# Zero fills, bias loads and the last image's attention reordered in a four-image vision-transformer kernel

## The chip, the cores and the metric

The kernel runs on one core of a Trainium2 chip. The metric is the device time of one execution in microseconds, the median of three runs. The core has engines with instruction streams of their own: TensorE (PE: matmuls and transposes, with weight loads PEld), VectorE (DVE), ScalarE (ACT), GpSimd (POOL) and SyncE (SP, which here only starts DMA transfers). An engine takes its instructions in order and waits at semaphores for the others.

## The reference

Four images of 3 x 224 x 224 pixels become 784 tokens each (patches of 8 x 8), of width 256, in float32:

```python
# tokenizer: patches -> (4, 784, 192)
tokens = layernorm(patches, ln1_g, ln1_b) @ W1 + b1
tokens = layernorm(tokens, ln2_g, ln2_b)
tokens = concatenate([tokens, tokens, tokens], axis=1)   # used 3 times
h = silu(layernorm(tokens @ Wp1 + bp1, lnp_g, lnp_b)) @ Wp2 + bp2
# layer 0: at each token position attention between the images, 8 heads of 32
mn = layernorm(layernorm(h)) * gamma + beta
q, k, v = mn @ Wq, mn @ Wk, mn @ Wv
g = sigmoid(mn @ Wg + bg)
att = softmax(einsum('slhc,tlhc->sth', q, k) * scale, axis=1)
h = h + (einsum('sth,tlhc->slhc', att, v) * g) @ Wo + bo
# layer 0: two experts of six per token, chosen by a router
x = layernorm(h)
p = softmax(relu(x @ router_w1 + router_b1) @ router_w2 + router_b2)
w = softmax(top2(p))
h = h + sum(w_e * (relu(relu(x @ w1_e + b1_e) @ w2_e + b2_e) @ w3_e + b3_e))
# layer 1: linear attention with W_qkv and W_out, then a shared MLP
# plus two experts of four per token
```

The shape of the tokens after the concatenation is (4, 2352, 256). As the three parts are equal, and as nothing tells them apart later, the kernel computes 784 rows for each image and writes each result three times. `s` and `t` number images: an image's query meets the keys of all four images, its products summed over all positions.

## The kernel before

An image has six tiles of 128 tokens and 16 left over; the 64 left over of all images make tile 24, so 25 tiles. `h` holds all tokens in SBUF throughout.

**Patch section** (lines 330 to 526). The pixels land in `img` (126 partitions: rows of patches). Per group `k` of four patch columns (7 groups), `flatten(k, put)` copies pixels into patch order (`vT`, L342); `patch_stats` takes batch-norm statistics from `img` on DVE (L448); `patch_stds` turns them into a root, written into `vT` by ACT (L459); `turn_patches(k, c)` transposes `vT` on PE into `ptp` (L352) and copies it to `pT` (L356), c=0 for the first 128 pixels of a patch, c=1 for the other 64 and the root. In between stand the pieces of a generator (`steps`, begun by `next`), which folds W1, the norms and Wp1 into one weight `Wall`: pwct and pw/pwc (matmuls), the copy to the second half of `Wall` (L430), its end with `lastf` (L432 to L438), and `bp1` added (L441). Last, `pc` (L525) transposes `stage`, the 46 rows of biases and gains that 13 small loads bring (L178), and `cols` (L526) keeps them as columns. The order of this section on each engine is written out by hand.

**Tokenizer** (L612 to 730). `tokenize(g)` and `first_steps(g)` take tiles in groups: `pw` (L622) multiplies a tile with `Wall` in one c=0 and one c=1 pass for each half, ACT copies it, DVE takes statistics, and so on.

**GpSimd's and SyncE's queues in the front.** GpSimd issues the load of `bp1`, the 13 loads of `stage`, then memsets (`pL` L335, `nothing` L553, `base0` L575, `table` L581 and L587, `blk` L592, `shift`), then loads bp2, bo, rb2. SyncE issues images and weights and then 46 DMAs which write `nothing` over `xrows` and `yrows` in DRAM (L557; up to 896 KB each, 41 MB in all); each has a manual dependency on `turned`, the copy to `cols`.

**Layer 0.** `products(s, o, ts)` multiplies queries of image s with keys (`kq`) on DVE (L884); `gate_mm` (pg), `gate_act`, `shares_before/after` (the softmax over the images), `first_value` and `values` (weighted sums of v, `oT`, L930) and `attended(s, two)` (pwo, L291, `h` L959) follow. Then per part of the tokens: `rows_of_part` and `turn_part` normalise and transpose (`xn`, `pt`), `router` and `router_logits` (pr, `rT` L1019, plg L1030), `choose` (top two, a run of small DVE instructions), `count` (pcount), `send` (positions, then GpSimd scatters the rows to `xrows`, ordered by expert, L1121). The parts are `past` (image 1), `u` (image 2), `ua` and `ub` (image 3's two halves).

**Expert blocks.** When the rows of enough images are counted, `early_blocks()` finds 7 full blocks of 256 rows that are already known (ptotal, pplace, pmeta: places, experts). `load(i)` fetches block i from `xrows` to `xb` (L1437, after the scatters), `own_weights(i)` copies its expert's weights out of `ew` (all six experts, 1,540 columns each) with an offset read from a register (L1456, L1458), `turned(i)` transposes (ptb), `hidden(i, k)` multiplies (pb, L1482), `rows_back(i)` gives pyb (L1500) and writes to `yrows`; later rows are fetched back and added.

**The last image** (L1517 to 1640) is a list written out by hand, in whose order the instructions of each engine stand; `manual_schedule(engines=by_hand)` names the engines for which that holds. `ew` takes the place of `kq` when the products are done, and is loaded by 6 DMAs of 768 KB, each for all experts:

```python
        for i, name in enumerate(("expert_w1", "expert_w2", "expert_w3")):
            for c in range(2):
                nc.sync.dma_start(
                    out=ew[:, :, (2 * i + c) * D : (2 * i + c + 1) * D],
                    in_=a[f"L0_ffn_{name}"].rearrange("e (c p) n -> c p e n", p=P)[c],
                )
        for i in range(4):
            load(i)
```

After it come the second layer's attention and MLPs, which are not touched.

Of the kernel before, what the change touches and what calls it, by code (L numbers as in the profile page):

```python
# [27 lines left out]
P = 128  # L28
TT = 128
# [43 lines left out]
def tile_vit_tower(ctx: ExitStack, tc: tile.TileContext, a: dict, out: bass.AP):  # L73
# [97 lines left out]
    img = tokp.tile([IP, CY, WID], F32, tag="img", name="img")  # L171
    bp1 = tokp.tile([TT, D], F32, tag="bp1", name="bp1")
    nc.gpsimd.dma_start(out=bp1, in_=a["L0_tok_bp1"].partition_broadcast(TT))
# [3 lines left out]
    for src, n, width in plan:  # L177
        nc.gpsimd.dma_start(out=stage[r0 : r0 + n, :width], in_=src)  # L178
        r0 += n
# [153 lines left out]
    pT = tokp.tile([P, 2, QP, HP], F32, tag="pT", name="pT")  # L333
    pL = tokp.tile([P, 2, NI, SEG], F32, tag="pL", name="pL")
    nc.gpsimd.memset(pL, 1.0)  # L335
# [4 lines left out]

    def flatten(k, put):
        put(  # L342
            flat[:, k * PW : (k + 1) * PW, :PD].rearrange("q w (y x) -> q w y x", x=PATCH),
            img[:, :, k * PW * PATCH : (k + 1) * PW * PATCH].rearrange(
                "q y (w x) -> q w y x", x=PATCH
            ),
        )

# [12 lines left out]
    def first_layers():  # L361
# [12 lines left out]
        bb = tokp.tile([P, 2, TT], F32, tag="bb", name="bb")  # L374
        W1g = tokp.tile([KP, 2, D], F32, tag="W1g", name="W1g")
        W2 = tokp.tile([P, 2, D], F32, tag="W2", name="W2")
# [36 lines left out]
        WcT = tokp.tile([P, 2, 2 * P], F32, tag="WcT", name="WcT")  # L413
# [16 lines left out]
        nc.vector.tensor_copy(Wall[:, :, D:], pp)  # L430
# [9 lines left out]
        )  # L440
        nc.vector.tensor_tensor(bp1, pw, bp1, ALU.add)  # L441
# [21 lines left out]
    Wall = tokp.tile([P, 2, 2 * D], F32, tag="Wall", name="Wall")  # L463
    perm = tokp.tile([KP, 2, 2 * P], F32, tag="perm", name="perm")
# [7 lines left out]
    with tc.manual_schedule(engines=by_hand):  # L472
# [19 lines left out]
        cut0 = 5  # L492
        flatten(0, nc.vector.tensor_copy)
# [4 lines left out]
        flatten(3, nc.vector.tensor_copy)  # L498
        flatten(2, nc.scalar.copy)
        turn_patches(1, 0)  # L500
        next(steps)
# [3 lines left out]
        flatten(4, nc.scalar.copy)  # L505
        next(steps)
        turn_patches(3, 0)
        flatten(5, nc.scalar.copy)
        turn_patches(4, 0)
        patch_stds(0, cut0)  # L510
        turn_patches(5, 0)
        flatten(6, nc.scalar.copy)
        for k in range(2):
            turn_patches(k, 1)
        turn_patches(6, 0)
        for k in range(cut0, NK):
# [27 lines left out]
    rb2 = spread(wts, "rb2", a["L0_ffn_router_b2"])  # L544
    for put in weight_loads:
# [6 lines left out]
    nothing = tokp.tile([P, 7 * D], F32, tag="nothing", name="nothing")  # L552
    nc.gpsimd.memset(nothing, 0.0)  # L553
    for r in range(0, XROWS, 7 * P):
        n = min(7, (XROWS - r) // P)
        for rows_ in (xrows, yrows):
# [5 lines left out]
                put.ins, turned.ins.name,  # L562
# [15 lines left out]
    NQ = QMAX * E0  # L578
    table = const.tile([1, 5, NQ], F32, tag="table", name="table")
    for q in range(QMAX):  # L580
        nc.gpsimd.memset(table[:, 0, q * E0 : (q + 1) * E0], float(BLK * q))  # L581
    by_e = table.rearrange("r k (q e) -> r k q e", e=E0)
    for e in range(E0):
        for k, v in (
            (1, CAP * e - DUMMY), (2, EW * e), (3, D * e), (4, CAP * e - DUMMY + SMALL)
        ):
            nc.gpsimd.memset(by_e[:, k, :, e], float(v))  # L587
# [1819 lines left out]
```

## Time and profile before

| what | before |
|---|---|
| median of 3 runs | 746.83 us (746.51 to 748.01) |
| profiled execution | 774.73 us, its span 773.0 us |
| busy: PE, PEld | 702.5 us (91%), 479.4 us (62%) |
| busy: DVE, ACT, POOL | 475.7 (62%), 333.9 (43%), 126.2 us (16%) |
| moved by DMA | 96.49 MB, mean 125 GB/s |

The profile is one execution and is 27.9 us (3.7%) longer than the median. Engine rows name the line, engine, operation, output and input, the busy time, and in brackets the idle time before it with what ended it. In the row of slices each digit is a fortieth of the span (19.3 us) in tenths of busy time; PEclk is the clock granted to TensorE in tenths of full speed. In a row of waits the three numbers are the sum, the count and the longest.

### The profile page before, as it was taken

What the parts mean: (1) busy time and instruction counts of PE and PEld (TensorE: products, weight loads), DVE (VectorE), ACT (ScalarE), POOL (GpSimd) and SP (SyncE); (2) the same over time, 40 slices, a digit from 0 to 9 for tenths busy, and PEclk for the clock granted to TensorE, in tenths of its full rate; (3) what the DMA queues carried; (4) which work ended last, traced back from release to release, by engine and by line L of the source; (5) the groups of instructions that cost most, each with busy time, mean ns of one, the idle gap of its engine ahead of it and who ended that gap; (6) DMA issues with size and microseconds to landing.
All of it is one profiled execution on the core that took longest, in us unless ns stands there. A gap on an engine that the chain in (4) does not pass through costs nothing.

```text
span 773.0 us, 9815 instructions
## 1 busy us (share of the span) xinstructions
PE 702.5 (91%) x3005; PEld 479.4 (62%) x3005; DVE 475.7 (62%) x1487; ACT 333.9 (43%) x794; POOL 126.2 (16%) x232
## 2 busy tenths in 40 slices
PE   6889889999977778998899998789999999999996
PEld 4546555666655566787788874547776765554553
DVE  5686785869987553456444767348986844444541
ACT  1565766556674552342222326325446422222221
POOL 7200000000074226400003026724000000000000
PEclk9999999999998889999999998879999999999999
DMA  5799997000022913422324252312000012322333
GB/s 177 232 426 424 426 424 312 1 0 1 0 82 90 376 72 117 136 82 77 95 90 123 96 158 69 96 34 70 7 0 1 5 27 94 97 60 89 106 113 106
DMA packets 56284, 96.49 MB, mean 125 GB/s; under 512 B 6504, under 2 KB 46158, under 8 KB 56232
## 3 DMA queue, kind: packets, MB, share of 16 engines
q1 hardware_dynamic: 49732, 79.68, 28.8%
q0 software_dynamic: 5600, 14.32, 6.1%
q10 hardware_dynamic: 900, 1.86, 0.8%
q8 instruction: 24, 0.39, 0.2%
q14 instruction: 28, 0.23, 0.1%
HBM read 30.75 MB, written 65.09 MB: 124 GB/s over the span
## 4 chain that ended last, share of the span: by engine, by line
PE 68%; DVE 17%; ACT 7%; issue 4%; DMA 2%; DVEq 1%; another core or an unknown queue 1%; ACTq 0%
PE pb L1482 11%; PE pe L280 6%; PE pyb L1500 5%; PE ps L280 4%; PE pqk L1948 4%; PE pkv L280 4%; PE pt L271 4%; PE pw L622 3%; PE ps L2357 3%; PE pwp L291 3%; PE pukx L2047 3%; PE pout L2127 3%; DVE oT L930 3%; PE pout L2132 3%; DMA img<-in_x_dram 2%
## 5 line engine op out<-in xcount | busy, mean ns | idle before, releaser
L1121 POOL DMA_INDIRECT xrows<-xn,pos x50 | 53.0, 1061 | 246.4 <-DVE nm L980 189.4
L1705 POOL DMA_INDIRECT ys<-yrows,pos x50 | 49.1, 982 | 160.4 <-DMA yrows<-yb 126.7
L1482 PE MATMUL pb<-xTb,own 128*128 128x256 f32 (+1 forms) x240 | 55.8, 378 | 11.7 <-DVE own L1458 6.9
L1488 ACT ACTIVATE hb<-pb,own 128x256 f32<-128x256 f32 (+1 forms) x74 | 33.6, 457 | 62.6 <-PE pb L1482 51.3
L1948 PE MATMUL pqk<-Wqkv,lxT 128*128 128x512 f32 x100 | 49.9, 646 | 6.6 <-issue 6.6
L1482 PEld LDWEIGHTS pb<-xTb,own 128*128 128x128 f32 x240 | 42.3, 197 | 20.1 <-ACT hb L1488 7.8
L1500 PE MATMUL pyb<-own,hb 128*128 128x256 f32 x216 | 52.7, 384 | 0.3 <-ACT hb L1488 0.2
L1482 PE MATMUL pb<-hb,own 128*128 128x256 f32 (+1 forms) x240 | 52.1, 359 | 0.9 <-DVE hb L1490 0.6
L280 PE MATMUL pe<-xT,eW 128*128 128x512 f32 (+1 forms) x112 | 46.0, 553 | 0.0
L1500 PEld LDWEIGHTS pyb<-own,hb 128*128 128x128 f32 x216 | 40.8, 193 | 6.6 <-ACT hb L1488 0.6
L1482 PEld LDWEIGHTS pb<-hb,own 128*128 128x128 f32 x240 | 40.6, 190 | 5.8 <-DVE hb L1490 1.0
L1506 DVE TENSOR_TENSOR yb<-pyb,eb 128x512 f32<-128x512 f32 (+1 forms) x30 | 19.1, 638 | 39.1 <-PE pyb L1500 26.5
L622 PE MATMUL pw<-Wall,pT 128*128 128x512 f32 (+1 forms) x96 | 42.7, 593 | 0.0
L1471 ACT COPY xTb<-ptb 128x512 f32<-128x512 f32 (+1 forms) x30 | 16.2, 542 | 59.3 <-PE ptb L1467 49.3
L271 PE MATMUL pt<-ident,xn 128*128 128x128 f32 x200 | 30.4, 284 | 10.6 <-DVE xn L648 6.5
L271 PEld LDWEIGHTS pt<-ident,xn 128*128 128x128 f32 x200 | 23.8, 143 | 25.4 <-issue 6.2
L1490 DVE TENSOR_SCALAR hb<-pb,own 128x256 f32<-128x256 f32 (+1 forms) x46 | 20.5, 446 | 28.7 <-PE pb L1482 19.6
L1948 PEld LDWEIGHTS pqk<-Wqkv,lxT 128*128 128x128 f32 x100 | 19.9, 207 | 28.6 <-issue 26.8
L884 DVE SCALAR_TENSOR_TENSOR prod<-kq 128x784 f32<-128x784 f32 x32 | 30.4, 970 | 6.1 <-ACT kq L1298 3.4
L280 PEld LDWEIGHTS pe<-xT,eW 128*128 128x128 f32 x112 | 20.2, 190 | 21.6 <-issue 16.5
L1458 DVE COPY own<-ew 128x1540 f32 x30 | 28.9, 965 | 7.0 <-issue 2.6
L622 PEld LDWEIGHTS pw<-Wall,pT 128*128 128x128 f32 (+1 forms) x96 | 17.9, 189 | 20.0 <-issue 17.9
(420 smaller groups left out, 1469.1 us busy)
## 6 DMA issues: line engine op xcount, KB each, us to landing
xrows<-nothing SPq DMA_DIRECT2D x22, 896.0 KB
yrows<-nothing SPq DMA_DIRECT2D x22, 896.0 KB
out_dram<-h SPq DMA_DIRECT2D x23, 384.0 KB
xb<-xrows SPq DMA_DIRECT2D x24, 256.0 KB
yrows<-yb SPq DMA_DIRECT2D x24, 256.0 KB
ew<-in_L_ffn_expert_w_dram SPq DMA_DIRECT2D x6, 768.0 KB
wb<-wd SPq DMA_DIRECT2D x16, 128.0 KB
img<-in_x_dram SPq DMA_DIRECT2D x5, 294.0 KB
```

The lines of the kernel that those rows point to most:

```text
L271: nc.tensor.transpose(pt[:, j * TT : (j + 1) * TT], xn[:, j, c * P : (c + 1) * P], ident[:TT, :TT])
L280: nc.tensor.matmul(pm[: wcols.stop - wcols.start, :n], w[:, c, wcols], xT(c), start=(c == 0), stop=(c == chunks - 1),)
L291: nc.tensor.matmul(pm[:, i, :], xT(c, t), w[:, c, :], start=(c == 0), stop=(c == chunks - 1))
L622: nc.tensor.matmul(pm, pixels(c, tiles[j]), Wall[: K1[c], c, :], start=(c == 0), stop=(c == 1))
L884: nc.vector.scalar_tensor_tensor(prod, qTs[s][:, o, :], 1.0, kT[:, o, t * SEQ : (t + 1) * SEQ], ALU.mult, ALU.mult, accum_out=atts[s][:, o ...
L1121: put = nc.gpsimd.indirect_dma_start(out=xrows[:, :], out_offset=bass.IndirectOffsetOnAxis(ap=pos[:, k, t0 + j : t0 + j + 1], axis=0), in_ ...
L1458: nc.vector.tensor_copy(w, ewf[0][:, bass.ds(off, EW)])
L1482: nc.tensor.matmul(pm, wm[:, c, o * P : (o + 1) * P], src[:, c, :], start=(c == 0), stop=(c == 1),)
L1488: nc.scalar.activation(dst[:, o, :], pm, AF.Relu, bias=b)
L1500: nc.tensor.matmul(pm[:, t, :], src[:, c, t * P : (t + 1) * P], wm[:, c, :], start=(c == 0), stop=(c == 1),)
L1705: got = nc.gpsimd.indirect_dma_start(out=y[:, j, k, :], out_offset=None, in_=yrows[:, :], in_offset=bass.IndirectOffsetOnAxis(ap=pos[:, k, ...
L1948: nc.tensor.matmul(pqk, xTs[u][:, c, cut(j, 1)], Wqkv[:, c, : 2 * D], start=(c == 0), stop=(c == 1),)
```

## The change

- GpSimd's memsets go ahead of the load of `bp1`; the tiles made before them are named earlier, so that `nothing` and the others keep their addresses. The 13 loads of `stage` go behind bp2, bo and rb2 on GpSimd's queue and wait for DVE's last copy of `flatten`.
- `pc` and the copy to `cols` go from the end of the patch section into the tokenizer, ahead of group 1 (on PE behind the eight pw of the first pair).
- Groups 0, 3 and 5 of `flatten` are on DVE (before: 0 and 3), the other four on ACT. The second half of `Wall` is copied by ACT (before: DVE), and the last `pT` by ACT (before: DVE). 8 and 10 transposes of the identity whose result is not used are added on PE.
- The 46 zero fills wait for the last statistics of the pixels, no longer for `cols`.
- Last image: both `gate_mm` stand ahead of the products; `early_blocks` is cut into more pieces, placed apart; `ew` is a view of `kq`, loaded in 18 DMAs of 256 KB by expert, of which the first 6 come behind `products(3, 0, [3])`; `load` 0 to 3 come behind the first values; `router(u)` comes ahead of the values; `turned(0)`, `own_weights(0)`, `hidden(0, 0)` and `own_weights(1)` come ahead of `choose(u)`; `count(u)` comes behind `router(ua)`.

```diff
@@ -169,13 +169,48 @@
...
+    pT = tokp.tile([P, 2, QP, HP], F32, tag="pT", name="pT")
+    bb = tokp.tile([P, 2, TT], F32, tag="bb", name="bb")
+    W1g = tokp.tile([KP, 2, D], F32, tag="W1g", name="W1g")
+    W2 = tokp.tile([P, 2, D], F32, tag="W2", name="W2")
+    WcT = tokp.tile([P, 2, 2 * P], F32, tag="WcT", name="WcT")
+    Wall = tokp.tile([P, 2, 2 * D], F32, tag="Wall", name="Wall")
+    perm = tokp.tile([KP, 2, 2 * P], F32, tag="perm", name="perm")
+    pL = tokp.tile([P, 2, NI, SEG], F32, tag="pL", name="pL")
+    nothing = tokp.tile([P, 7 * D], F32, tag="nothing", name="nothing")
+    nc.gpsimd.memset(nothing, 0.0)
+    base0 = const.tile([TT, E0], F32, tag="base0", name="base0")
+    for e in range(E0):
+        nc.gpsimd.memset(base0[:, e : e + 1], float(CAP * e))
...
-        nc.gpsimd.dma_start(out=stage[r0 : r0 + n, :width], in_=src)
+        small_loads.append(nc.gpsimd.dma_start(out=stage[r0 : r0 + n, :width], in_=src))
...
@@ -330,21 +365,22 @@
...
-    pT = tokp.tile([P, 2, QP, HP], F32, tag="pT", name="pT")
-    pL = tokp.tile([P, 2, NI, SEG], F32, tag="pL", name="pL")
-    nc.gpsimd.memset(pL, 1.0)
...
+    flattened = []
...
-        put(
+        done = put(
...
+        if put != nc.scalar.copy:
+            flattened.append(done.ins.name)
...
@@ -427,7 +459,8 @@
...
-        nc.vector.tensor_copy(Wall[:, :, D:], pp)
+        nc.scalar.copy(Wall[:, :, D:], pp)
+        yield
...
@@ -438,6 +471,7 @@
...
         )
+        yield
         nc.vector.tensor_tensor(bp1, pw, bp1, ALU.add)
...
@@ -490,41 +522,40 @@
...
         cut0 = 5
+        next(steps)
+        for _ in range(8):
+            nc.tensor.transpose(warm[:, :P], ident, ident)
         flatten(0, nc.vector.tensor_copy)
...
             patch_stats(k)
-        flatten(3, nc.vector.tensor_copy)
         flatten(2, nc.scalar.copy)
         turn_patches(1, 0)
+        for k in (3, 5):
+            flatten(k, nc.vector.tensor_copy)
         next(steps)
...
         flatten(4, nc.scalar.copy)
+        turn_patches(3, 0)
+        flatten(6, nc.scalar.copy)
+        for k in range(4, NK):
+            turn_patches(k, 0)
         next(steps)
-        turn_patches(3, 0)
-        flatten(5, nc.scalar.copy)
-        turn_patches(4, 0)
+        for _ in range(10):
+            nc.tensor.transpose(warm[:, :P], ident, ident)
         patch_stds(0, cut0)
-        turn_patches(5, 0)
-        flatten(6, nc.scalar.copy)
-        for k in range(2):
+        for k in range(cut0):
             turn_patches(k, 1)
-        turn_patches(6, 0)
         for k in range(cut0, NK):
             patch_stats(k)
-        for k in range(2, cut0):
+        next(steps)
+        patch_stds(cut0, NK)
+        for k in range(cut0, NK):
             turn_patches(k, 1)
-        patch_stds(cut0, NK)
         next(steps)
-        turn_patches(5, 1)
-        turn_patches(6, 1, nc.vector.tensor_copy)
-        pc = ps_tile("pc")
-        nc.tensor.transpose(pc[:, :nrows], stage, ident[:nrows, :nrows])
-        turned = nc.vector.tensor_copy(cols, pc[:, :nrows])
     Wp2 = tokw.tile([P, 2, D], F32, tag="Wp2", name="Wp2", bufs=1)
...
@@ -542,6 +573,12 @@
...
+    for put in small_loads:
+        tc.add_manual_dep(
+            put.ins, flattened[-1],
+            mybir.DependencyInfo(mybir.DependencyClass.Sync, mybir.DependencyReason.DATA),
+            reason="behind the copies",
+        )
...
@@ -549,8 +586,6 @@
...
-    nothing = tokp.tile([P, 7 * D], F32, tag="nothing", name="nothing")
-    nc.gpsimd.memset(nothing, 0.0)
...
@@ -559,7 +594,7 @@
...
             tc.add_manual_dep(
-                put.ins, turned.ins.name,
+                put.ins, arrived[-1],
                 mybir.DependencyInfo(mybir.DependencyClass.Sync, mybir.DependencyReason.DATA),
...
@@ -570,29 +605,6 @@
...
-    base0 = const.tile([TT, E0], F32, tag="base0", name="base0")
-    for e in range(E0):
-        nc.gpsimd.memset(base0[:, e : e + 1], float(CAP * e))
...
-    nc.gpsimd.memset(shift, 0.0)
-    nc.gpsimd.memset(shift[:, 0, :], float(DUMMY))
...
@@ -704,6 +716,10 @@
...
             second_rows(0, second_norm(0))
+        if g == 1:
+            pc = ps_tile("pc")
+            nc.tensor.transpose(pc[:, :nrows], stage, ident[:nrows, :nrows])
+            nc.vector.tensor_copy(cols, pc[:, :nrows])
         tokenize(g)
...
@@ -827,6 +843,7 @@
...
+    ew = kq[:, : E0 * EW].rearrange("p (e n) -> p e n", e=E0)
...
@@ -961,6 +978,8 @@
...
+        if block is not None:
+            turned(block)
...
@@ -1159,11 +1178,16 @@
...
-        meta = small.tile([1, 3, n], I32, tag=f"meta{n}", name="meta", bufs=1)
+        return pm, small.tile([1, 3, n], I32, tag=f"meta{n}", name="meta", bufs=1)
+    def meta_out(pm, meta, n):
...
+    def meta_of(these, place, n):
+        return meta_out(*meta_mm(these, place, n), n)
...
@@ -1176,10 +1200,16 @@
...
-        place = numbered(full)
+        pp = psum_s.tile([P, 512], F32, tag="pss", name="pplace")[:NQ, :1]
+        nc.tensor.matmul(pp, before[:NQ, :NQ], full, start=True, stop=True)
+        yield
+        place = small.tile([NQ, 1], F32, tag="place", name="place", bufs=1)
+        nc.vector.tensor_copy(place, pp)
...
-        metas[0] = meta_of(full, place, NEARLY)
+        pm, meta = meta_mm(full, place, NEARLY)
+        yield
+        metas[0] = meta_out(pm, meta, NEARLY)
...
@@ -1337,12 +1367,22 @@
...
+    def expert_weights(es):
+        for e in es:
+            for i, name in enumerate(("expert_w1", "expert_w2", "expert_w3")):
+                nc.sync.dma_start(
+                    out=ew[:, e, 2 * i * D : 2 * (i + 1) * D].rearrange("p (c n) -> p c n", c=2),
+                    in_=a[f"L0_ffn_{name}"][e].rearrange("(c p) n -> p c n", p=P),
+                )
     def added_rows(s):
...
             products(s, 0, [NI - 1])
+            if s == NI - 1:
+                expert_weights(range(2))
             choose(past)
...
@@ -1391,7 +1431,7 @@
...
-    with tc.manual_schedule(engines=by_hand):
+    with tc.manual_schedule(engines=by_hand | {ENG.SP}):
...
@@ -1517,81 +1557,76 @@
     s = NI - 1
     past, u, ua, ub = (s - 2, 0, TPI), (s - 1, 0, TPI), (s, 0, GT), (s, GT, TPI + 1 - GT)
     rest = (GN, SEQ - GN)
-    with tc.manual_schedule(engines=by_hand):
+    with tc.manual_schedule(engines=by_hand | {ENG.SP}):
+        gate_mm(s, 0)
+        gate_mm(s, 1)
         products(s, 1, [1])
+        expert_weights([2])
         scales_of(u)
         send(past)
         steps = early_blocks()
         next(steps)
-        gate_mm(s, 0)
         shifts_of(u)
         products(s, 1, [2])
         next(steps)
+        gate_act(s, 0)
         products(s, 1, [3])
+        expert_weights(range(3, E0))
         next(steps)
-        gate_act(s, 0)
         mx = shares_before(s)
-        gate_mm(s, 1)
-        for _ in steps:
-            pass
+        next(steps)
         gate_act(s, 1)
         shares_after(s, mx)
     att.close()
     work[0] = layer0.enter_context(tc.tile_pool(name="blocks", bufs=2, reuse_waits="tile"))
-    ew = keys.tile([P, E0, EW], F32, tag="kq", name="ew")
-    ewf[0] = ew.rearrange("p e n -> p (e n)")
+    ewf[0] = kq[:, : E0 * EW]
     eb3 = work[0].tile([P, E0 * D], F32, tag="eb3", name="eb3", bufs=1)
     nc.gpsimd.dma_start(
         out=eb3, in_=a["L0_ffn_expert_b3"].rearrange("e n -> (e n)").partition_broadcast(P)
     )
     with tc.manual_schedule(engines=by_hand | {ENG.SP}):
-        for i, name in enumerate(("expert_w1", "expert_w2", "expert_w3")):
-            for c in range(2):
-                nc.sync.dma_start(
-                    out=ew[:, :, (2 * i + c) * D : (2 * i + c + 1) * D],
-                    in_=a[f"L0_ffn_{name}"].rearrange("e (c p) n -> c p e n", p=P)[c],
-                )
-        for i in range(4):
-            load(i)
         first_value(s, 0, 0, GN, nc.vector)
         first_value(s, 1, 0, GN, nc.scalar)
         rows_of_part(u)
         mix1(past)
         values(s, 0, 0, GN)
+        for _ in steps:
+            pass
+        for i in range(4):
+            load(i)
         values(s, 1, 0, GN)
         turn_part(u)
         mix2(past)
         for o in range(2):
             first_value(s, o, *rest, nc.scalar)
+        router(u)
         values(s, 0, *rest, range(1, 3))
         attended(s, [0, 1])
         values(s, 0, *rest, range(3, NI))
         attended(s, [2, 3])
         mix3(past)
+        scales_of(ua)
         values(s, 1, *rest)
         keep_left(s)
-        router(u)
-        scales_of(ua)
         router_logits(u)
-        attended(s, [4, 5])
         shifts_of(ua)
-        rows_of_part(ua)
-        attended(s, [6])
         for i in (0, 1):
             b = cols[:, rows[f"eb{i + 1}_0"] :][:, : 2 * E0].rearrange("p (e r) -> p e r", r=2)
             nc.vector.tensor_copy(ew[:, :, 6 * D + 2 * i : 6 * D + 2 * i + 2], b)
+        attended(s, [4, 5], 0)
+        own_weights(0)
+        rows_of_part(ua)
+        attended(s, [6])
+        hidden(0, 0)
+        turn_part(ua)
+        own_weights(1)
+        scales_of(ub)
         choose(u)
-        turned(0)
-        turn_part(ua)
-        own_weights(0)
-        scales_of(ub)
-        count(u)
-        hidden(0, 0)
+        turned(1)
         shifts_of(ub)
         rows_of_part(ub, both=True)
-        own_weights(1)
-        turned(1)
         router(ua)
+        count(u)
         send(u)
         hidden(0, 1)
         turn_part(ub, both=True)
```

More of the change, by code (lines that the diff above doesn't have):

```diff
@@ L171, in tile_vit_tower @@
     img = tokp.tile([IP, CY, WID], F32, tag="img", name="img")
+    pT = tokp.tile([P, 2, QP, HP], F32, tag="pT", name="pT")
[11 more added lines that the diff above has]
+        nc.gpsimd.memset(base0[:, e : e + 1], float(CAP * e))
+    NQ = QMAX * E0
+    table = const.tile([1, 5, NQ], F32, tag="table", name="table")
+    for q in range(QMAX):
+        nc.gpsimd.memset(table[:, 0, q * E0 : (q + 1) * E0], float(BLK * q))
+    by_e = table.rearrange("r k (q e) -> r k q e", e=E0)
+    for e in range(E0):
+        for k, v in (
+            (1, CAP * e - DUMMY), (2, EW * e), (3, D * e), (4, CAP * e - DUMMY + SMALL)
+        ):
+            nc.gpsimd.memset(by_e[:, k, :, e], float(v))
+    for k in (1, 4):
+        nc.gpsimd.tensor_tensor(table[:, k, :], table[:, 0, :], table[:, k, :], ALU.add)
+    blk = const.tile([NQ, NBLK], F32, tag="blk", name="blk")
+    for i in range(NBLK):
+        nc.gpsimd.memset(blk[:, i : i + 1], float(i))
+    shift = const.tile([1, 3, NBLK], F32, tag="shift", name="shift")
+    nc.gpsimd.memset(shift, 0.0)
+    nc.gpsimd.memset(shift[:, 0, :], float(DUMMY))
+    nc.gpsimd.memset(pL, 1.0)
     bp1 = tokp.tile([TT, D], F32, tag="bp1", name="bp1")
+    small_loads = []
     nc.gpsimd.dma_start(out=bp1, in_=a["L0_tok_bp1"].partition_broadcast(TT))
@@ L373, in first_layers @@
         g1, g2 = (lambda i: gb[:KP, 2 * i : 2 * i + 1]), (lambda c: gb[:, 4 + c : 5 + c])
-        bb = tokp.tile([P, 2, TT], F32, tag="bb", name="bb")
-        W1g = tokp.tile([KP, 2, D], F32, tag="W1g", name="W1g")
-        W2 = tokp.tile([P, 2, D], F32, tag="W2", name="W2")
         m1 = tokp.tile([KP, 2], F32, tag="m1", name="m1")
@@ L412, in first_layers @@
         yield
-        WcT = tokp.tile([P, 2, 2 * P], F32, tag="WcT", name="WcT")
         pt = ps_tile("pwct").rearrange("p (f k) -> p f k", f=2)
@@ L461, in patch_stds @@
         )
-    Wall = tokp.tile([P, 2, 2 * D], F32, tag="Wall", name="Wall")
-    perm = tokp.tile([KP, 2, 2 * P], F32, tag="perm", name="perm")
     srow = tokp.tile([1, P], F32, tag="srow", name="srow")
@@ L572, in tile_vit_tower @@
     nc.vector.tensor_scalar(spare, spare, dead, None, ALU.mult)
-    base0 = const.tile([TT, E0], F32, tag="base0", name="base0")
-    for e in range(E0):
-        nc.gpsimd.memset(base0[:, e : e + 1], float(CAP * e))
[L578 to L587, printed above, removed]
-    for k in (1, 4):
-        nc.gpsimd.tensor_tensor(table[:, k, :], table[:, 0, :], table[:, k, :], ALU.add)
-    blk = const.tile([NQ, NBLK], F32, tag="blk", name="blk")
-    for i in range(NBLK):
-        nc.gpsimd.memset(blk[:, i : i + 1], float(i))
-    shift = const.tile([1, 3, NBLK], F32, tag="shift", name="shift")
-    nc.gpsimd.memset(shift, 0.0)
-    nc.gpsimd.memset(shift[:, 0, :], float(DUMMY))
     pTf = pT.rearrange("p c q w -> p c (q w)")
@@ L943, in keep_left, with attended @@
         nc.vector.tensor_copy(oL[:, :, s, :LEFT], oTs[s][:, :, TPI * TT :])
-    def attended(s, two):
+    def attended(s, two, block=None):
         if s not in sums:
@@ L1152, in numbered, with meta_mm @@
         return place
-    def meta_of(these, place, n):
+    def meta_mm(these, place, n):
         here = small.tile([NQ, NBLK], F32, tag="here", name="here", bufs=1)[:, :n]
```

## The prediction

> **What bounds the kernel now.** I read the page first (busy shares, the slices, the chain), then the order of time in the two stretches that the diff touches, then their waits, windows and DMA.
>
> ```profile
> PE   6889889999977778998899998789999999999996
> PEclk9999999999998889999999998879999999999999
> DMA  5799997000022913422324252312000012322333
> PE 68%; DVE 17%; ACT 7%; issue 4%; DMA 2%; DVEq 1%; another core or an unknown queue 1%; ACTq 0%
> ```
>
> TensorE sets the time: 702.5 us busy of 773.0, 68% of the chain. An edit that takes a wait from PE is worth that wait; one on another engine is worth nothing unless PE waits for it. The weak slices are the first (0 to 19 us) and the twelfth to sixteenth (213 to 309 us, with a lower clock): both are touched. The front, from the timeline:
>
> ```profile
> 16.66 0.61 DVE L342 COPY vT<-img 126x768 f32<-126x768 f32 x1 [3.20 <-DMA img<-in_x_dram]
> 17.19 2.16 DVE L448 BATCH_NORM_STATS2 pst<-img 126x6 f32<-126x192 f32 x8
> 19.27 2.02 DVE L342 COPY vT<-img 126x768 f32<-126x768 f32 x1
> 29.30 0.33 ACT L459 ACTIVATE vT<-pv,eps 126x8 f32<-126x8 f32 x1
> 29.68 1.07 PE L352 MATMUL ptp<-ident,vT 126*65 126x126 f32 x8 [0.84 <-ACT vT L459]
> 30.79 0.62 DVE L356 COPY pT<-ptp 65x448 f32<-65x448 f32 x1 [1.19 <-PE ptp L352]
> 30.87 3.71 PE L622 MATMUL pw<-Wall,pT 128*128 128x512 f32 x8
> ```
>
> The pixels land at 16.4; the tokenizer's first matmul goes at 30.87, and its second half needs the copy that ends at 31.41. Behind it lies the chain DVE statistics, ACT root (29.30), transposes, copies. Now the last image's attention, from the chain and the windows (columns: stretch, then busy of PE, PEld, DVE, ACT, POOL, granted clock, DMA share, GB/s):
>
> ```profile
> 240.10 0.39 PE ptotal L1141 x2
> 240.49 4.21 PE pg L280 x8
> 264.53 0.58 ACT rT L1019
> 265.16 2.73 PE plg L1030 x12
> 277.78 0.96 DVE own L1458
> 278.89 3.75 PE pb L1482 x8
> ...
> 240.00:260.00 20.00, 16.82 (x60) 10.76 (x61) 10.92 (x29) 11.09 (x25) 13.22 (x13) 0.83 0.73 254
> 260.00:280.00 20.00, 12.18 (x50) 9.56 (x50) 12.05 (x56) 10.21 (x26) 0.00 (x0) 0.77 0.66 233
> 280.00:300.00 20.00, 17.03 (x75) 13.06 (x73) 6.90 (x26) 5.93 (x13) 12.26 (x12) 0.89 0.31 106
> ...
> SPq L1437 <- DMA xrows<-xn,pos: 4.0, 1, 4.0
> ```
>
> In 260 to 280 no engine is over 61% busy: a run of waits. PE waits 3.25 us before ptotal, 3.89 before plg, 1.77 before pb, and the first expert block (pb) starts only at 278.89, behind choose(u) and own_weights. Half-clock pace shows beside them: pg takes 0.54 us a matmul where it takes 0.33 at full clock, plg's twelve take 2.73.
>
> **Part 1, zeros and bias loads on GpSimd.** Removed from 16.95 to 22.9: the memsets (nothing 1.59, table 0.49 + 1.00, blk 1.35). They go to about 4.3 to 10.8, and the bias loads L178 (13 at 0.52) go behind bp2, bo, rb2, waiting for DVE's copy k=5. What this takes off DVE: the copy at 19.27 took 2.02 where its twin took 0.61; that is 1.4. What it may put on: the memsets now lie beside DVE's preparation of Wall (W1g, W2). **The skill** ("SBUF — State Buffer", Who interferes with whom) says that a VectorE copy in a two-port mode and a GpSimd instruction exclude each other for a whole instruction. The 2.02 row agrees, and against the change it would make each such VectorE operation at 6 to 11 pay again: two at 1.4 is 2.8. By the row alone, that is one copy lengthened, by the rule 1.5 to 3. I take nothing: PE stands idle 14.74 to 17.33 before the pixels, and 2.6 of delay fits there, less 1.7 to 2.5 that the pwct and idle transposes now take. Bounds 0 to 2, by the rule a sum of 10.9 for the 12.9 below. bp1's own load slips from 4.29 to about 10.5 on POOL; its add stands at 29.
>
> **Part 2, the pixel copies.** Before: 2 on DVE, 5 on ACT at a 0.73 pitch; now 3 and 4. ACT loses one copy (0.73) and the 3.3 of idle that it had within 16.6 to 30.9 shrinks; it gains the Wall half (0.6). Stepping through by hand with the rows' durations: DVE copies to 17.2, 8 statistics to 19.3, copies 3 and 5 (0.55 each) to 20.4, 12 to 23.5, 8 to 26.2, Wall's end (1.0) to 27.1, second root arithmetic to 27.7; ACT's copies and c=0 evictions (0.43 pitch) end at 24.6, Wall 25.1, five c=1 evictions at 28.3, root 28.6, last two evictions 30.2. PE's last transposes end at 29.5, and the pw pair is whole at about 31.6 where it was 32.8: gain 1.2, bounds -0.5 and 2. The 18 idle transposes (18 x 0.11 to 0.21 = 2 to 3.8) stand where PE waits for the pixels and for ACT: nothing; if that cover is gone, at most 1 of it shows.
>
> **Part 3, cols and the zero fill.** pc (0.26) and its copy (0.19) move behind the eight pw of the first pair, wanted at about 33.8. The loads issue from 20.4, 0.52 each, to about 27.5 (each ninth waits for the first's landing). bp2, the nearest row, took 4.4 from issue to landing (22.85 to 27.25): last one at 32, slack 1.8. Under the pixels they took 8.0 to 8.9 (issued 5.42, waited for at 13.44): 36.4, a stall of 2.6. The 46 zero fills no longer wait for cols (31.33) but for the last statistics (26.2), so they run over these loads:
>
> ```profile
> q0 software_dynamic: 117, 0.66, 81.2%
> q1 hardware_dynamic: 140, 0.13, 19.2%
> ```
>
> These are packets, MB and share of two queues that both had work at 261 to 263 us: near one packet of one per packet of the other. A 512-byte row between 7168-byte ones (0.27 us each) then loses 0.3. The skill ("DMA: Bandwidth & Descriptors", Queues, rings and completion order) speaks against the change: a ring is drained for some 9 to 17 descriptors before the next has its turn, so a load may wait 17 x 0.27 = 4.6, and land at 36.6: a stall of 2.8, or 7.4 with two turns. The counts fit both. I take 0 and keep 7.4, by the rule a sum of 5.5. Behind the loads' new wait stand on POOL only oL's memset (0.30) and, after 210, the scatters. The fill itself ends some 5 earlier, worth nothing: the first scatter comes after 210.
>
> **Part 4, the last image.** Front to back, each against its own place before.
> - gate_mm(3,0) and (3,1) fill PE's hole 236.85 to 240.1 at full clock (16 x 0.33 = 5.2, to 242.1), so ptotal and pplace come at 242.7, where pplace stood at 244.53; products(3,1,[3]) ends 243.65 against 245.86: 2.2. With pg out of the way before shares, the softmax over images ends at 245.6 against 248.6: 3.0.
> - values: o=0 249.2, o=1 252.4 (255.2 before): 2.8. meta's add goes behind values(0): 249.4 against 246.7, later by 2.7, but the loads behind it on SP had to wait for send(past)'s scatters till 262.04 anyway.
> - Expert weights: 6 DMAs of 768 KB, issued 245.93 to 255.5, the last landing near 273, become 18 of 256 KB, the first six at 230; SP had stood waiting there for 127.6 us (behind place), with nothing else queued. At the 340 to 430 GB/s of this stretch 4.7 MB takes 12: all there at 252 to 256. The bias copies into ew (272.88 before) and own_weights lose their wait. On SP only the xb loads stand behind; they issue at 257.6 instead of 262.04 and land at 260.
> - router(u) before pwo: pr at 251 to 253.3, rT 255.1, so plg comes at 255.5 instead of 265.16, beside the values: the wait of 3.89 is gone. DVE's 5.29 wait for pwo[4,5] shrinks with it; PE then waits some 2 for DVE's values(1).
> - pwo[4,5] at 261.4; ptb(0) 262; own(0) 264.5; pb(0,0) 264.6 against 278.86, as it no longer stands behind choose(u) (273.02 to 276.66). own(1) 267.1, choose(u) to 270.8. pb(0,1) 271.2 (285.67), pb(1,0) 274.4 (288.84), pyb(0) 276.1 (290.67): 14.2 to 14.6.
> - send(u): 272.5 against 281.9, only 9.4, since two own copies (0.96 and a load of the register, 2.2 together) stand ahead of choose(u). Its scatters (12 x 1.27) and the two later batches have gaps of 3.59 and 4.55 on POOL, which take up the missing 5.
>
> Off this: PE waits some 4.8 for shares and values at 242.5 to 247.3, and about 2 at 260. The clock was halved in eight stretches of 3.4 to 6.8 between 226 and 305; one more such stretch costs half of 3.4, so 1.7; two cost 3.4. I take 2.7. Net 14.4 - 2.7 = 11.7. Ends: all idle (14) and half-clock loss (7) of 236.5 to 300 gone, 20; only send(u)'s 9.4 less 3.4, 6.
>
> **The sum.** 1.2 + 0 + 11.7 = 12.9 in the profiled execution, which took 774.73 (span 773.0), 3.7% over the median 746.83. Divided by 1.037: 12.4, less a margin of 0.4 for waits of semaphores that I set at nothing: 12.0. That gives 734.8.
>
> **The rivals.**
> - *GpSimd or the clock keeps half of it.* For: send(u) moves only 9.4, and half-clock stretches follow each hole. Against: POOL's two gaps. Gain 5 to 8: 740.
> - *The loads are starved at pc.* One mechanism, one place: SP's fill of 41 MB begins while the last five bias loads are on their way; TensorE is in order, so pc and all of the tokenizer behind it stand still, and DVE's copy with it. Decides from a last landing later than 33.8 + 12.9 = 46.7: that is four turns of 4.6 behind 28.2. If the loads waited for the fill's end (near 118) it would cost 84. A fifth turn lands at 51.2: a stall of 17.4 less 12.9 is 4.5 slower, 751. For: the page's rule and 8-us landings under load. Against: the counts 117 to 140.
> - *It does not do what it says*: xb or ew are late as before, since send(past) or another wait holds SP. Then the head part stays at about 3: 743 to 745.
>
> **How the numbers follow.** The main case (730 to 738) 0.55; half of it 0.22; hardly any of it (742 to 745) 0.09; starved loads or another late wait ahead of the whole kernel, ending slower, 0.11; within 0.2% (1.5 us, about what can be told from no change) 0.03. So faster 0.86, same 0.03, slower 0.11. The range leaves out a tenth on each side: 728 (a gain of 19, near the upper end of part 4) to 747.
>
> **What would show it.** Right: no copy vT<-img over 0.8 us on DVE; first pw near 29.5; pc without a wait; PE's wait before ptotal gone, plg before 260, pb(0,0) near 265, last ew landed before 257, scatters of u from 273. Wrong: PE idle ahead of pc with the last stage load as releaser; own waiting on ew; PE clock at a half through 245 to 280.

## The result, and the profile after

The changed kernel takes 735.32 us (median of 4 runs, 733.9 to 736.34) where the kernel before takes 746.67 beside it: a ratio of 0.9844, with a 95% interval of 0.9823 to 0.9866, or 11.35 us less. The forecast was 734.8.

One thing must be known to read the numbers below. The chips on which the runs fell are of two kinds. On two of them (call them S) the kernel before takes 771 to 773; where it was timed, and on another (call them F), 746 to 747. Each of these chips was used in one sitting only, so that it is not shown whether the kind belongs to the chip or to the hour. The profile of before that the prediction reads, 774.73 us, looks like S; its times, and the profile after (733.9, span 732.2), are of F. So the two profiles can't be subtracted from each other. A clean trace of the old order is that of n1 below (F; the kernel before without 26 of its 50 scatters, 745.68 against 745.89 for the whole kernel).

The page after, busy share and granted clock in slices (of 18.3 us here), and below it the same of n1 (slices of 18.6):

```profile
PE   7889899999998879997899998999999999999996
PEclk9999999999999899999999999999999999999999
...
PE   6889899999987879998799998999999999999996
PEclk9999999999998879999999999999999999999999
```

The slices of 7 in the last image (the twelfth to sixteenth) are one in place of two, and the clock is below 9 in one slice in place of three. The profile of before has four and six such slices, but part of that is S. The front, from the timelines after:

```profile
6.89 2.51 DVE L415 TENSOR_SCALAR W1g<-W,m,gbT 96x256 f32<-96x256 f32 x2
15.39 0.56 DVE L376 COPY vT<-img 126x768 f32<-126x768 f32 x1 [1.13 <-DMA img<-in_x_dram]
17.95 1.01 DVE L376 COPY vT<-img 126x768 f32<-126x768 f32 x2
...
16.18 1.91 PE L527 MATMUL pwarm<-ident 128*128 128x128 f32 x8
17.89 1.23 PE L388 MATMUL ptp<-ident,vT 126*128 126x126 f32 x8
29.01 1.07 PE L388 MATMUL ptp<-ident,vT 126*65 126x126 f32 x8 [0.83 <-ACT vT L493]
29.92 4.49 PE L634 MATMUL pw<-Wall,pT 128*128 128x512 f32 x10
```

No copy takes 2.02 us any more (two take 1.01; the one that took 2.02 took 1.14 in n1), and the first pw comes at 29.92, in n1 at 30.57. But pwct and the eight idle transposes now hold PE until 17.89, with the first copied pixels ready at 15.95. The last image, TensorE's timeline after, and the windows:

```profile
240.16 0.24 PE L1160 MATMUL ptotal<-ones,often 128*78 128x1 f32 x2
244.89 3.65 PE L306 MATMUL pt<-ident,xn 128*128 128x128 f32 x12 [1.59 <-ACT xn L1014]
255.40 1.40 PE L1049 MATMUL plg<-rw,rT 128*128 128x6 f32 x12
259.14 1.56 PE L326 MATMUL pwo<-Wo,oT 128*128 128x256 f32 x6 [1.80 <-DVE oT L952]
264.42 1.97 PE L1522 MATMUL pb<-xTb,own 128*128 128x256 f32 x8 [2.17 <-DVE own L1498]
...
240.00:260.00 20.00, 14.63 (x67) 10.70 (x66) 16.11 (x52) 14.09 (x34) 12.43 (x13) 0.83 0.77 264
260.00:280.00 20.00, 17.64 (x94) 14.07 (x93) 11.91 (x50) 11.76 (x28) 5.98 (x6) 1.00 0.46 157
280.00:300.00 20.00, 19.68 (x109) 17.44 (x108) 10.92 (x43) 7.80 (x17) 15.43 (x16) 1.00 0.51 173
```

No wait is left ahead of ptotal and plg; 1.80 stand ahead of pwo, and 2.17 ahead of the first block (own). In n1 the same rows are:

```profile
239.72 0.40 PE L1141 MATMUL ptotal<-ones,often 128*78 128x1 f32 x2 [3.24 <-DVE often L1139]
251.11 0.33 PE L271 MATMUL pt<-ident,xn 128*128 128x128 f32 x1
...
262.16 1.60 PE L1030 MATMUL plg<-rw,rT 128*128 128x6 f32 x12 [1.27 <-ACT rT L1019]
263.62 3.56 PE L291 MATMUL pwo<-Wo,oT 128*128 128x256 f32 x8
274.93 3.75 PE L1482 MATMUL pb<-xTb,own 128*128 128x256 f32 x8 [1.77 <-DVE r L979]
...
240.00:260.00 20.00, 16.94 (x60) 10.59 (x61) 13.82 (x41) 11.71 (x27) 13.22 (x13) 0.84 0.75 262
260.00:280.00 20.00, 14.82 (x60) 11.34 (x59) 10.86 (x49) 10.76 (x26) 0.00 (x0) 0.76 0.64 225
```

The first block starts 10.5 us earlier after the change (264.42 against 274.93), and TensorE runs at full clock in 260 to 280 where it had 0.76. Starts in the traces, in us (yb is the addition that ends a block; pe begins the second layer's MLP):

| | profile of before (S) | e0 (S) | e4 changed (S) | n1 (F) | changed (F) |
|---|---|---|---|---|---|
| first pw | 30.87 | 30.38 | 30.30 | 30.57 | 29.92 |
| first y copied | 32.90 | 32.40 | 32.25 | 32.59 | 31.87 |
| first pkv | 108.58 | 108.12 | 110.66 | 108.24 | 108.23 |
| first pb | 278.89 | 278.36 | 271.07 | 274.93 | 264.42 |
| yb of block 0 | 294.22 | 292.16 | 285.14 | 288.56 | 277.25 |
| yb of block 3 | 319.47 | 318.24 | 319.29 | 309.04 | 297.80 |
| first pqk | 464.49 | 461.81 | 465.75 | 452.55 | 441.60 |
| first pe | 631.45 | 624.67 | 630.33 | 601.92 | 590.97 |

On F the lead of 10.5 to 11.3 at the first blocks is still 10.95 at pqk and pe. It is nearly the whole of the 11.35. On S the lead of 7.0 at block 0 (e4 against e0, two chips of that kind) has turned into a lag of 1.0 at block 3. The yb of block 3 stands at 315.9 to 321.0 in all nine traces of S, those of the runs below included, whatever was moved ahead of it.

### The profile page after: what moved, and what is told of

The parts are those of the page before. It is cut to its first block, busy times and chain, and to the rows that moved or that the text cites. A ratio compares the mean times of both kernels' runs of the same rounds, so it can differ in the third digit from the quotient of the medians.

```text
span 732.2 us, 9873 instructions
## 1 busy us (share of the span) xinstructions
PE 683.9 (93%) x3023; PEld 470.4 (64%) x3023; DVE 475.1 (65%) x1486; ACT 333.1 (45%) x795; POOL 126.4 (17%) x232
## 4 chain that ended last, share of the span: by engine, by line
PE 53%; DVE 6%; ACT 2%; issue 2%; DMA 1%; DVEq 1%; SPq 0%; ACTq 0%
PE pb L1522 12%; PE pe L315 6%; PE pyb L1540 5%; PE ps L315 5%; PE pqk L1983 4%; PE ps L2392 3%; PE pout L2162 3%; PE pout L2167 3%; PE pukx L2082 2%; PE pt L306 2%; PE pe L2362 2%; PE ps L2386 2%; DVE own L1498 1%; PE ptb L1507 1%; PE pkvo L2142 1%
## 5 line engine op out<-in xcount | busy, mean ns | idle before, releaser
L1522 PE MATMUL pb<-xTb,own 128*128 128x256 f32 (+1 forms) x240 | 52.8, 363 | 9.2 <-DVE own L1498 8.0
L1528 ACT ACTIVATE hb<-pb,own 128x256 f32<-128x256 f32 (+1 forms) x74 | 33.8, 457 | 53.4 <-PE pb L1522 46.5
L1522 PEld LDWEIGHTS pb<-xTb,own 128*128 128x128 f32 x240 | 40.6, 190 | 17.0 <-ACT hb L1528 6.4
L1983 PE MATMUL pqk<-Wqkv,lxT 128*128 128x512 f32 x100 | 44.9, 594 | 0.2 <-ACT lxT L94 0.2
L1530 DVE TENSOR_SCALAR hb<-pb,own 128x256 f32<-128x256 f32 (+1 forms) x46 | 20.5, 446 | 27.9 <-PE pb L1522 21.2
L1498 DVE COPY own<-kq 128x1540 f32 x30 | 28.8, 963 | 7.8 <-ACT xTb L1511 2.6
L1997 ACT ACTIVATE qk<-qk 128x256 f32<-128x256 f32 x50 | 20.4, 408 | 22.9 <-DVE qk L1989 20.8
L1983 PEld LDWEIGHTS pqk<-Wqkv,lxT 128*128 128x128 f32 x100 | 18.4, 190 | 19.3 <-issue 17.0
```

The source lines that it names most:

```text
L1498: nc.vector.tensor_copy(w, ewf[0][:, bass.ds(off, EW)])
L1522: nc.tensor.matmul(pm, wm[:, c, o * P : (o + 1) * P], src[:, c, :], start=(c == 0), stop=(c == 1),)
L1528: nc.scalar.activation(dst[:, o, :], pm, AF.Relu, bias=b)
L1983: nc.tensor.matmul(pqk, xTs[u][:, c, cut(j, 1)], Wqkv[:, c, : 2 * D], start=(c == 0), stop=(c == 1),)
```

## The experiments

Ratios are to the kernel before beside them on the same chip. First, on S, the kernel before once more (no edit), and the two halves of the change by themselves.

> The kernel before once more, for a second profile. The profile of before took 774.73 us against a median of 746.83, with half-clock stretches at 264 to 284 and at 479 to 520 us and a slower second layer. Theory A (those are accidents of that one execution): this profile takes 745 to 750, the stretches from the last block result (yb) to the end last about 291 us as in the changed kernel (before: 309), and the lead of the changed kernel is 10 to 13 us at that point. Theory B (the reordered last image also spares the kernel the later half-clock stretches): they come again at the same places and the second layer again lasts some 309 us.

Measured: 768.01 (one run; others of before beside it have a median of 771.03). Theory A falls as it was put: the slower second layer comes again (163.5 us from the last yb to pe; 167.6 in the profile of before, 150.0 in the changed kernel on F). It is not an accident of one execution, but it is not the kernel's order either, since e4 below shows it for the changed kernel, so B falls as well: it goes with the chip, or with the hour.

```diff
 e1_front: the changed kernel's front (hunks up to the tokenizer), the last image of before
 e2_last:  the front of before, the changed kernel's last image
```

> Only the front of the change (parts 1 to 3: zeros and bias loads, pixel copies, idle transposes, cols, zero fill); the last image as before. The prediction's step: 1.2 us faster than before (bounds -0.5 to 2); the changed kernel's profile has its first pw 0.95 earlier than before, so 745.7. Rival (the front is worth nothing and the last image is all): 746.5 to 747.

Measured: 770.45 against 771.03, ratio 0.9980 (0.9957 to 1.0003): no difference that can be told; but the interval reaches to 3.3 us of gain, so that the forecast's 1.2 is not excluded by it. First y at 32.41 against 32.40, first pkv at 108.83 against 108.12.

> Only the last image's part of the change (part 4); the front as before. The prediction's step: 11.7 in the profile, 11.3 on the median's scale, so about 735.5; if front and last image add up to the measured 11.35 with 1 from the front, 736.4. Rival (the front carries the gain): over 742.

Measured: 770.51, ratio 0.9987 (0.9969 to 1.0005). Neither theory: block 0 ends at 280.87, 11.3 ahead of e0, as the step says, and block 3 at 317.56, 0.7 ahead. The row in which most of the lead goes, the yb of block 1, from DVE's timeline of e2 (in e0 it comes at 305.15):

```profile
303.28 0.69 DVE L1530 TENSOR_TENSOR yb<-pyb,eb 128x512 f32<-128x512 f32 x1 [14.58 <-remote]
```

Its input, pyb, had been there since 288.9, and "remote" says that the profile finds no instruction of this core that released it.

Then the place of the first block, by itself:

```diff
-        attended(s, [4, 5], 0)
-        own_weights(0)
+        attended(s, [4, 5])
         rows_of_part(ua)
         attended(s, [6])
-        hidden(0, 0)
-        turn_part(ua)
-        own_weights(1)
-        scales_of(ub)
         choose(u)
-        turned(1)
+        turned(0)
...
```

> The changed kernel, but turned(0), own_weights(0), hidden(0, 0), own_weights(1), turned(1) and count(u) stand behind choose(u) in the order of before. If the gain lies in the first expert block no longer standing behind choose(u): choose takes 3.7 us and the block's chain 2, so 3 to 5 us slower than the changed kernel (739 to 741), pb(0,0) in the trace at 268 to 270 in place of 264.4. Rival (the early gate matmuls, weights and router bring it all, the place of choose nothing): within 1 us of 735.3.

Measured: 764.73, ratio 0.9904 (0.9875 to 0.9933), on the chip of e0 to e2. First pb at 273.38. The changed kernel was not run on this chip, so that the expectation, which is against it, can't be judged here; on the other S chip it came out as follows.

> The changed kernel unaltered, beside the kernel before on the chip on which the parts were run (there before takes 771, and its trace shows stops of ACT and DVE of 3 to 15 us that no semaphore explains, while GpSimd issues its scatters and gathers). Theory A (the gain is the change's own and the stops hit both kernels alike): ratio 0.984, about 759, with such stops in its trace too. Theory B (front and last image only gain together, because the scatters then fall where they stop nobody): 745 or less, no stop in the trace. Theory C (the stops eat the gain, as they did in the last image's part alone): 765 to 771.

Measured: 773.27 against 772.8, ratio 1.0012 (0.9993 to 1.0031): theory C. On S the change is worth nothing. Its trace at 289 to 298, DVE, ACT and GpSimd:

```profile
297.29 0.18 DVE L1129 TENSOR_TENSOR at<-pcount,base 128x24 f32<-128x24 f32 x1 [7.98 <-remote]
...
290.89 0.47 ACT L1528 ACTIVATE hb<-pb,own 128x256 f32<-128x256 f32 x1 [2.68 <-PE pb L1522]
297.35 0.84 ACT L1528 ACTIVATE hb<-pb,own 128x256 f32<-128x256 f32 x2 [5.99 <-remote]
...
293.08 0.96 POOL L1140 DMA_INDIRECT xrows<-xn,pos  x1 [0.30 <-issue]
294.35 0.96 POOL L1140 DMA_INDIRECT xrows<-xn,pos  x1 [0.30 <-issue]
```

`at` needs only pcount, which PE issued at 289.17 for 0.40; it starts 7.7 us after that ended. ACT stands still for 6 and resumes within 0.1 of it, after the last scatter of the batch (294.35). The order in which these engines' instructions stand in the program gives no cause for it.

Two more edits of the changed kernel went along on that chip. One puts both gate_mm(3, ...) back behind ptotal and behind shares_before; the other puts, in the program, all of expert_weights behind products(3, 1, [3]).

> The changed kernel, but both gate matmuls of the last image stand where they stood before (behind ptotal, and behind the sums of the softmax). The prediction's step: ptotal 2 to 3 us later, the softmax 3.0 later, so 2 to 3.5 us slower than the changed kernel beside it. Rival (DVE's weighted sums or the register loads set the end, the gates are covered): within 1 us of it.

Measured: 776.33, 3.06 over e4's 773.27; ratio to before 1.0057 (1.0031 to 1.0084). The size is what was expected, but the trace does not support the step: a stop of 6.53 ("remote") stands at meta, 257.52, on top of the gates, and e4 and e6, whose order is the same (below), lie 1.48 apart. Inconclusive.

> The changed kernel, but all 18 loads of the expert weights stand behind the last product of the last image (issued from about 241.6 in place of 230.3). The prediction's step: the loads are 4.7 MB, 12 us at 390 GB/s, all there at 255 to 257, ahead of the bias copies at 259.9: no loss, within 1 us of the changed kernel. Rival (the early loads carry the first block): 3 to 8 us slower, own waiting for ew in the trace.

Measured: 771.79, 1.48 less than e4; ratio 0.9974 (0.9950 to 0.9997). But the edit delayed nothing. SyncE's queue in e6, and below it in the changed kernel on F:

```profile
217.49 2.68 SPq L1373 DMA_DIRECT2D kq<-in_L_ffn_expert_w_dram  x4
230.95 8.21 SPq L1373 DMA_DIRECT2D kq<-in_L_ffn_expert_w_dram  x5
241.34 7.18 SPq L1373 DMA_DIRECT2D kq<-in_L_ffn_expert_w_dram  x9
...
216.84 2.68 SPq L1373 DMA_DIRECT2D kq<-in_L_ffn_expert_w_dram  x4
230.31 8.21 SPq L1373 DMA_DIRECT2D kq<-in_L_ffn_expert_w_dram  x5
240.69 5.66 SPq L1373 DMA_DIRECT2D kq<-in_L_ffn_expert_w_dram  x9
```

SyncE has nothing else queued there, so the loads are the next thing in its queue from either place, and they start as parts of `kq` come free (in e6 a product ends at 241.23, and the next load starts at 241.34). Four of the first six start at 217, earlier than the forecast's 230. So e6 is the changed kernel once more; what the early loads are worth was not tried, and the 1.48 shows how far two runs of one order can lie apart here. Two rows bear on it. The first own waits 1.60 in e4 and e6 and 1.59 in the changed kernel on F, with another DMA named each time, so that the weights don't seem to be what it waits for. And in n1, where the weights are issued from 245.55, the DMA engines move 350 to 400 GB/s until 272 (other loads included), while the changed kernel's first own starts at 263.31: with the loads as before it might have waited.

The bias loads, without their wait, at 11 to 22 us beside the pixels:

```diff
-    for put in small_loads:
-        tc.add_manual_dep(put.ins, flattened[-1], ...)
```

> The changed kernel, but the 13 small bias loads no longer wait: they stand behind the load of bp1 on GpSimd's queue, at about 11 to 20 us, beside the pixels. Theory A (the pixels landed 1.1 us earlier in the changed kernel because these loads are out of their way, and that was the front's gain): the first pixel copy moves from 15.4 to 16.0 or later, 0.6 to 1.3 us slower than the changed kernel. Rival B (pixels land when they do, the gain is the copies on DVE): first copy at 15.4, within 0.3 us.

Measured: 772.15, ratio 0.9987 (0.9959 to 1.0015), 1.1 less than e4, not more. The first pixel copy did come late, at 17.87; but with the loads out of the way it comes at 17.79 (e4), 17.50 (e5), 16.83 (e6), 15.84 (e3) and 15.39 (changed kernel, F). Theory A falls: the arrival wanders by 2.4 us whatever these loads do. And it hardly matters: first y came at 32.25 in e4 and at 31.87 after the change on F, 0.38 apart for pixels 2.4 apart, since with early pixels PE is held by its own pwct and idle transposes.

The last four leave out the scatters of images 2 and 3 (26 of the 50: 24 are left in the traces; the expectations speak of 38), in the kernel before (n1), in the changed one (n2), in it with the first block behind choose(u) (n3, the edit of e3), and in it with router(u) behind the values (n4):

```diff
-        for j in range(n):
+        for j in range(n if b < 2 else 0):
             for k in range(2):
                 put = nc.gpsimd.indirect_dma_start(
...
-        router(u)
         values(s, 0, *rest, range(1, 3))
...
         keep_left(s)
+        router(u)
         router_logits(u)
```

> The kernel before, without the 38 scatters of images 2 and 3 to xrows (rows of these images are not sent, so their experts see zeros); everything else stays. Theory A (GpSimd's unbroken train of scatters at 272 to 324 us is what ACT and DVE stop behind on these chips, and pins the fourth block result near 318): the stops at 280 to 325 vanish, the fourth yb comes at 308 to 313, 5 to 9 us faster than before. Rival B (the stops have nothing to do with the scatters): stops as before, within 2 us of it.

Measured: 745.68 against 745.89, ratio 1.0000 (0.9988 to 1.0011). This chip is an F: the whole kernel's time leaves no room for the stops there either, and so the question put to n1 got no answer. What it does show: where nothing stops, 26 scatters cost nothing.

> The changed kernel, without the same 38 scatters. Theory A: with the train gone, the lead that the reordered last image has at the first block result (7 to 11 us here, 17 where it was timed) is kept: 10 to 14 us faster than the kernel before without these scatters, fourth yb at 297 to 302. Rival B (the lead is lost for another reason, such as the clock or the order of the later blocks): within 4 us of the kernel before without these scatters.

Measured: 736.54, ratio 0.9882 (0.9864 to 0.9899), 9.1 less than n1. Fourth yb at 299.62 against 309.04. This repeats the gain on another chip of kind F, a little smaller than the 10 to 14 expected.

> The changed kernel without the 38 scatters, and with the first expert block behind choose(u) as it stood before. The prediction's step: choose (3.7 us) and what comes with it stands ahead of the first block again: 3 to 5 us slower than the changed kernel without these scatters, pb(0,0) 4 to 6 later. Rival (the place of choose is worth nothing once the scatters are gone; with them the same edit was 8 us faster than the changed kernel): within 1.5 us.

Measured: 740.69, 4.15 over n2; ratio 0.9926 (0.9910 to 0.9942). First pb at 271.05 in place of 265.09. The step holds here. On S the same edit (e3, 0.9904) came out better against before than the changed kernel (e4, 1.0012), on two different chips.

> The changed kernel without the 38 scatters, and with router(u) behind the last image's values, as it stood before. The prediction's step: plg again waits for pr and the copy behind it (3.9 us of waiting, and 2.6 of pr no longer beside the values): 3 to 6 us slower than the changed kernel without these scatters. Rival (TensorE then does pwo first, and the waits only change places): within 1.5 us.

Measured: 740.61, 4.07 over n2; ratio 0.9930 (0.9917 to 0.9942). PE's timeline of n4 shows the wait come back, and first pb at 268.57:

```profile
254.43 2.74 PE L315 MATMUL pr<-xT,rw 128*128 128x512 f32 x8
259.18 2.06 PE L1049 MATMUL plg<-rw,rT 128*128 128x6 f32 x12 [2.00 <-ACT rT L1038]
261.09 3.76 PE L326 MATMUL pwo<-Wo,oT 128*128 128x256 f32 x8
```

## Why the prediction was right, and where not

**The last image carries it, through the waits named.** Forecast 11.7 in the profile, measured 10.5 (first pb) to 10.95 (pe). The place of choose and the place of router, each undone alone, cost 4.15 and 4.07 of n2's 9.1. That leaves about 1 for the gates, the front and the weights together only if the parts add up, and the rows above speak against it: the changed kernel leads n1 by 6.2 at pt (244.89 against 251.11), ahead of both of those steps, by 4.5 at pwo (259.14 against 263.62), where PE waits for DVE's values, and by 10.5 at pb. The lead at pt comes where both gates have been moved ahead; what they are worth at the end was not shown, for only the chip with stops measured them, and the weights' part was not tried.

**Its terms were mis-sized, and the errors cancel.** The 14.2 to 14.6 were read off a profile in which own, pb and pyb came late: first pb at 278.89, in n1 at 274.93, so 3.9 of it did not exist on F. Most of it is a pause of ACT and DVE, as the same row shows in the profile of before and in n1:

```profile
259.51 1.04 DVE L930 SCALAR_TENSOR_TENSOR oT<-vT,att,oT 128x272 f32<-128x272 f32 x2 [3.63 <-ACT oT L923]
...
256.51 1.04 DVE L930 SCALAR_TENSOR_TENSOR oT<-vT,att,oT 128x272 f32<-128x272 f32 x2 [1.01 <-ACT oT L923]
```

The rest is half clock at plg (2.73 against 1.60). In the other direction the forecast took off 2.7 for half-clock stretches; there were fewer, not more. (The profile of before has six of them between 226 and 305, not eight; four are of 3.4 and two of 6.8.) In 225 to 290 n1 has 20.4 us at half clock (five stretches of 3.4 and 6.8, as its windows 0.84 and 0.76 show), the changed kernel 6.8, n2 10.2. In these traces half-clock stretches went with the waits; that is part of the 10.5, not a loss beside it. The forecast counted 3.9 that was not there, took off 2.7 that was not lost, and added 1.2 for a front that did not last; it is in part luck that 734.8 lies 0.5 from 735.32.

**Dividing by 1.037 was wrong in kind.** The profile's 27.9 us over the median are not spread over the span. Against n1 it is 3.9 late at the first pb, 11.9 at pqk and 29.5 at pe: but for the 3.9, the excess lies in the later blocks and in the second layer's attention, behind all that the change touches. Here that cost only 0.5.

**The front: 0.7 of the 1.2 came, and none of it lasted.** The first y came 0.7 earlier on F (31.87 against 32.59), inside the bounds. Part 1's copy of 2.02 was not what the tokenizer waited for. It took 1.14 in n1, 0.63 in e0 and 0.69 in e2, and in all four traces of the old front DVE had the second root's operands 1.5 us or more before ACT, busy with evictions, ran the root (in n1 26.67 and 29.00). By the fifth y copy 0.4 of the lead had been paid back, where pc now stands among the pw passes. This is a step of part 3 that failed: pc and its copy were costed at nothing, as moved; but they were taken from a place ahead of the first pw, and what PE saves there it pays later in its own queue. The rest went at 55 to 61, in n1 and then after:

```profile
57.42 4.22 PE L291 MATMUL pwp<-Wp,xTt 128*128 128x256 f32 x16
61.47 7.04 PE L622 MATMUL pw<-Wall,pT 128*128 128x512 f32 x16
...
56.79 4.84 PE L326 MATMUL pwp<-Wp,xTt 128*128 128x256 f32 x16
61.47 7.04 PE L634 MATMUL pw<-Wall,pT 128*128 128x512 f32 x16
```

A half-clock stretch stands in both, to 58.6 in n1 and to 59.3 after, so that more of pwp falls into it; both start the next pw at 61.47, and at pkv nothing is left (108.23 against 108.24). The other traces agree: first pkv comes at 107.71 to 110.66 in the ten with the new front and at 108.12 to 109.70 in the four with the old. On F the front was not run by itself.

**GpSimd's memsets beside DVE.** Part 1 left open whether DVE's operations would be lengthened by 1.5 to 3, by the rule of the Trainium skill that it cites ("SBUF — State Buffer", Who interferes with whom). They were: two W1g took 2.51 where they took 0.73, so 1.8, and the same in all ten traces with the new front. pwc starts at 8.58 in place of 7.80, and with pwct and the idle transposes PE comes to the pixels 1.9 after the first copy is ready (17.89 against 15.95). The cover did not hold where the pixels are early; whether these 1.9 reach the end was not tried.

**The loads under the zero fill.** The last stage load was issued at 29.2, not 27.5 (GpSimd waited 1.1 to 1.5 three times for an earlier load), and took, from the stage tile of the trace after,

```profile
DMA to landing us min/median/max: 5.3/6.3/7.3
```

so by the median it landed near 35.5, later than the 33.8 at which pc was said to be wanted. No stall came of it, because pc stands behind 16 passes, not eight, and is issued at 36.92. Two misreadings that cancel. The landings are about 2 over bp2's 4.4: more than the count of packets gives (0.3), less than the 4.6 that the prediction estimates for one whole turn by the rule of the skill's "DMA: Bandwidth & Descriptors" (Queues, rings and completion order). The rival was close: an estimated 1.4 us of slack by the median landing, 0.4 by the longest.

**The rivals.** GpSimd's train of scatters did not keep half of it on F: it ran from 272.49 to 307.3 without a gap such as the 3.59 and 4.55 before, and PE's lead over n1 is still whole behind it (the sixth yb comes at 312.10, in n1 at 323.15). On S the gain went to nothing, in the blocks beside that train; the forecast had this outcome only as "half", and put down to send(u).

**What stays open.** Why ACT and DVE stop on S. Most of the stops lie in the stretches where GpSimd issues indirect transfers back to back (272 to 325, and the gathers at 480 to 540), and some end with a batch; n1 was to test whether they go with the scatters, and fell on F. Whether e3's order is better on S because its scatters leave gaps was not tried either, and e3 and e4 ran on different chips of that kind. (Its pauses are shorter: 6.58 and 6.32 ahead of the first two yb, in n1 2.62 and 2.68.) What the early weights and the front bring on F is open too. Of the versions run, the changed kernel is the fastest on F and e3 on S; none was shown to be fastest on both.

## What to carry to other kernels

Look whether a profile is of the same kind as the times: when it is 4% longer than the median, find where the excess lies before any row of it is turned into a gain, and don't spread it. On an engine that sets the end, undo each move alone: here undoing either of two moves of whole steps ahead of a wait cost some 4 us, while a front that was ready 0.7 earlier brought nothing that lasted. Look in the trace whether an undoing took place: a DMA moved in the program stayed where it was, since nothing else stood in its queue. A gain can vanish on another chip; compare versions on several.

## What the runs showed of the hardware that was not expected

The same program took 735.32 on one chip and 773.27 on another, and the kernel before 746.67 and 772.8: the ratio, not only the time, differed (0.9844 against 1.0012, intervals apart). On the slower kind single instructions of ACT and DVE wait as long as 14.6 us (e2), in e4 with both engines resuming within 0.1 us of each other (297.29 and 297.35), and the profile names no instruction of this core that released them.

Taking 26 of 50 scatters away, some 33 us of GpSimd's time at 1.27 from one to the next, changed the time by 0.2 us on a chip without stops.
